# A sort's pieces placed anew, Exp for both router functions, and ScalarE multiplying more rows of a slot table

## The chip, the cores and the metric

The kernel runs on one core of a Trainium2 chip. The metric is the device time of one execution in microseconds (us); the median of several executions is given. A core has five engines that run side by side, each with a queue of its own that is worked off strictly in order: TensorE (PE: matmuls and transposes, results into PSUM), VectorE (DVE), ScalarE (ACT: functions and scaled copies), GpSimd (POOL) and SyncE (SP, which here issues DMAs). An engine waits on semaphores for what others produce. PSUM has eight banks of 128 x 512 float32; which matmul may start is often a matter of which bank has been read out.

## The reference, cut to what matters

One block: a layer norm of x (8 sequences of 512 tokens, 512 wide), then two branches on the normed tokens, whose results are multiplied and added to x.

```python
xn = _layernorm(x)
s = attention(xn)          # 16 heads of 32, chunks of 128, gated group norm, output matmul
g = silu(mixture(xn))      # 16 experts, 4 per token, and one shared expert
return x + s * g

# attention: q, k = rotate(silu(xn @ Wq)), rotate(silu(xn @ Wk)); v = xn @ Wv
#   per chunk: scores = (q @ k.T) * decay; o = scores @ v + (q * decay_q) @ state
#   o = o * sigmoid(xn @ Wg1 @ Wg2); o = o * rsqrt(mean(o*o per head) + eps) * weight; o @ Wo
# mixture:
probs = softmax(xn @ gate_w.T)
routing_weights, selected = top_k(probs, 4)
routing_weights /= routing_weights.sum(-1, keepdims=True)
for e in range(16):
    mixed += comb[:, e:e+1] * (silu(xn @ Wg[e]) * (xn @ Wu[e])) @ Wd[e]
mixed + swiglu_shared(xn) * sigmoid(xn @ shared_gate_w)
```

## The kernel before, in words

All is float32. The program is one long trace that is laid out in stages; a scheduler places each engine's instructions by its own estimate of when they become ready, except where the code ties an instruction behind an earlier one (`on_pe()` ties every matmul group of the first stages behind the one before, so PE's order is the order of the code; `behind(engine)` ties an instruction behind the engine's latest).

- **First pass** (`first`, sequences b = 0 to 7): norm, transposes (`turn`, psT L289), router logits (`route_1` to `route_3`: plT, pl, lg, the four largest, wt and the one-hot masks `mask`), and the shared expert (`share_1`: pg in bank m and pu in bank d, L355; `share_2`: pys L371, copied by ACT at L374 and stored). It is a generator. `along()` draws nine fifths of a piece each time it is called, so that the first pass runs between the steps of the attention of sequence 0. When its pieces end, the first piece of `sort` runs.
- **PSUM banks** are named by tags: a has four, d two, m one, k one. A tile of a tag takes the bank of that tag that was taken longest ago and waits until it has been read. Keys (`key`: pk L659, Silu at L669, rotation on DVE at L671 to L675) take m, queries take d, `value(b, t)` takes m for even t and d for odd t (pv L615, copied at L619), scores take the four a banks.
- **sequence(b)** is the attention of one sequence: for each of four groups of heads `scores` (pk of the states L714, ps L725, masked on DVE into sc at L750), `step()`, key of group g + 2 (or two value tiles of the next sequence), `by_token` (transposes of kT, L691, scaled by ACT into kd, L696), `step()`, query, `output` (po L766 and L772, multiplied on DVE at L776). After the groups: the last value tile, `squares` (ACT, PE's pr, square root rs), `inverse` (reciprocal on DVE, L794), keys and queries of the next sequence, `normed` (pb, on at L810), and for sequence 0 the output matmul `project` (pw L817, in bank d, copied by ACT into so at L1029). `also()` draws a piece of `sort` in sequence 0.
- **sort**: where each token's four rows go among the blocks of the experts. Piece 1: two matmuls (total, before) that sum the masks, L387. Piece 2: a scan and some thirteen small DVE instructions (L393 to L428). Piece 3: nine more (L432 to L450), which give `at`. Then four pieces, each a POOL product (oa, L456) and a DVE sum (pos, L458). The last piece makes posi and sp, the softmax weights wt (Exp on ACT, L470; product with the mask on POOL, L471; den and its reciprocal on DVE, L473 and L474; product on POOL, L475), and the Sigmoid of the shared gate sgs (L477), and stores them.
- **table**: turns positions into slots, in 8 groups of 16 lists. `make(i)` compares on DVE, in two halves of 8 lists: places (L526, 128 x 512 float16) and blocks (L529). The places must be multiplied by a token number: the first half on DVE in one instruction (L533), the second half by ACT, one instruction of 128 x 64 for each list (`number`, L542). Two homes hold two groups, so that a group is made while the one before it is used. PE multiplies 16 pairs per group into pn (L565, bank a), DVE adds pn to acc (L576, L574). `between[0]` draws a piece of the table after each matmul of sequence 1's keys, queries and values. The last part sums up pslot (L581), and DVE writes the slots (L586), by which POOL gathers rows for the expert blocks (L1153).
- **gate_2** makes the gate of the next `on` (p L645, four tiles in four banks; Sigmoid on ACT, L649). In sequence 1 it runs in group 0.
- Then come the expert blocks (304 to 692 us) and the attention of sequences 2 to 7 with the mixture.

Of the kernel before, what the change touches and what calls it, by code (L numbers as in the profile page):

```python
# [10 lines left out]
F32 = mybir.dt.float32  # L11
# [4 lines left out]
AF = mybir.ActivationFunctionType  # L16
ALU = mybir.AluOpType
AX = mybir.AxisListType
# [79 lines left out]
def tile_block(ctx: ExitStack, tc: tile.TileContext, a: dict, out: bass.AP):  # L98
# [8 lines left out]
    def bank(tag, name):  # L107
        return pp.tile([P, 512], F32, tag=tag, name=name, bufs={"a": 4, "k": 1, "m": 1, "d": 2}[tag])
# [110 lines left out]
    def behind(engine):  # L219

        last = next(
            (i for i in reversed(nc.cur_bb.bb.instructions) if i.engine == engine), None)
        return tc.issue_after(last) if last else nullcontext()
# [140 lines left out]
    def share_2(b):  # L364
        h = h1_of.pop(b)
        xT1_of.pop(b)
        for t in range(NC):
            sh = p1.tile([P, D], F32, tag="sh1", name=f"sh1_{b}_{t}", bufs=6)
            py = bank("dama"[t], f"pys_{b}_{t}")
            with on_pe():  # L370
                nc.tensor.matmul(  # L371
                    py, lhsT=h[:, t * P : (t + 1) * P], rhs=sw[:, KC * 2 * F :],
                    start=True, stop=True)
            nc.scalar.copy(sh, py)  # L374
            nc.sync.dma_start(sh_d[b][t * P : (t + 1) * P, :], sh)


    def sort():
# [5 lines left out]
        for to, by, name in ((total, ones, "total"), (af, tri, "before")):  # L384
            ps = bank("a", f"p{name}")
            with on_pe():
                nc.tensor.matmul(ps, lhsT=by, rhs=mf, start=True, stop=True)  # L387
            nc.scalar.copy(to, ps)
        yield
        incl = p1.tile([P, E, NT], F32, tag="incl", name="incl")  # L390
        fl = incl.rearrange("p e t -> p (e t)")
# [34 lines left out]
            nc.vector.tensor_scalar(end[:, 1], end[:, 1], float(2 * PAIRS), None, ALU.add)  # L426
        with behind(DVE):
            nc.vector.tensor_copy(filled, end[:, 1, E - 1 : E])  # L428
        yield

        with behind(DVE):
# [35 lines left out]
        with behind(DVE):  # L467
            nc.vector.tensor_copy(sp, bl.rearrange("p w r t -> p w (r t)"))

        nc.scalar.activation(wt, wt, AF.Exp)  # L470
        nc.gpsimd.tensor_tensor(wt, wt, mask.rearrange("p e t -> p t e"), ALU.mult)  # L471
        den = p1.tile([P, NT], F32, tag="den", name="den")
        nc.vector.tensor_reduce(den, wt, axis=AX.X, op=ALU.add)  # L473
        nc.vector.reciprocal(den, den)  # L474
        nc.gpsimd.tensor_tensor(  # L475
            wt, wt, den.unsqueeze(2).to_broadcast([P, NT, E]), ALU.mult)
        nc.scalar.activation(sgs, sgs, AF.Sigmoid)  # L477
        nc.sync.dma_start(sg_d, sgs)
        nc.sync.dma_start(
            xn_d[:, 2 * D :].rearrange("(t p) e -> p t e", p=P),  # L480
# [5 lines left out]
    def table(room):  # L486

        half = room.bitcast(F16)  # L490
        free = [0]
        quads = GROUP // QUAD


        def part(*shape):
            n = int(np.prod(shape))
            free[0] += n
            flat = half[:, free[0] - n : free[0]]
            return flat.rearrange("p (q j) -> p q j", j=QUAD) if len(shape) == 2 else (
                flat.rearrange("p (u q j) -> p u q j", u=quads, j=QUAD))  # L500

        homes = [(part(quads, HALF, QUAD), part(quads, 2 * NB, QUAD))]
        free[0] = 2 * WE * (LATE - LATE // 2)
        homes.append((part(quads, HALF, QUAD), part(quads, 2 * NB, QUAD)))

        def flat(n):
            free[0] += n
            return half[:, free[0] - n : free[0]]

        acc = flat(2 * NB)  # L510

        def rows(of, n):
            return of.rearrange("p (u j) -> p u j", j=QUAD).unsqueeze(2).to_broadcast(
                [P, of.shape[-1] // QUAD, n, QUAD])

        def make(i):
            place, block = homes[i // GROUP % 2]
            for u in range(0, quads, quads // 2):
                us = slice(u, u + quads // 2)
                lists = slice(i + u * QUAD, i + (u + quads // 2) * QUAD)  # L520

                def counts(n):
                    return count[:, :n].unsqueeze(1).to_broadcast([P, quads // 2, n, QUAD])

                with tc.issue_after(masked[0]) if i == GROUP and u == 0 else nullcontext():
                    nc.vector.tensor_tensor(  # L526
                        place[:, us], counts(HALF), rows(sp[:, 0, lists], HALF), ALU.is_equal)
                with tc.issue_after(masked[0]) if i == GROUP and u == 0 else nullcontext():
                    nc.vector.tensor_tensor(  # L529
                        block[:, us], counts(2 * NB), rows(sp[:, 1, lists], 2 * NB),  # L530
                        ALU.is_equal)
                if u == 0:
                    nc.vector.tensor_tensor(  # L533
                        place[:, us], place[:, us], rows(half_token[:, lists.start % NT :][
                            :, : GROUP // 2], HALF), ALU.mult)

        def number(i, some):
            place = homes[i // GROUP % 2][0]
            for j in range(max(some[0], GROUP // 2), some[1]):
                row = place[:, j // QUAD, :, j % QUAD]  # L540
                t = (i + j) % NT
                nc.scalar.activation(row, row, AF.Copy, scale=token[:, t : t + 1])  # L542

        yield
        make(0)
        for j in range(0, GROUP, 4):
            number(0, (j, j + 4))
            yield
        for i in range(0, TOPK * NT, GROUP):
            more = i + GROUP < TOPK * NT  # L550
            if more:
                make(i + GROUP)
            else:
                for e in range(E - LATE, E - LATE // 2):
                    nc.sync.dma_start(wexp[:, e, :], a["experts"][:, e, :])
            if i < TOPK * NT // 2:
                yield
            place, block = homes[i // GROUP % 2]
            pn = bank("a", f"pn_{i}")
            for some in ((0, 5), (5, 10), (10, GROUP)):  # L560
                if some[0] == 5:
                    with on_pe():
                        for j in range(GROUP):
                            h = j % 2 * HALF
                            nc.tensor.matmul(  # L565
                                pn[h : h + HALF, : 2 * NB],
                                lhsT=place[:, j // QUAD, :, j % QUAD],
                                rhs=block[:, j // QUAD, :, j % QUAD], start=(j < 2),
                                stop=(j >= GROUP - 2))
                if more:  # L570
                    number(i + GROUP, some)
                if some[1] == GROUP:
                    if i:
                        nc.vector.tensor_tensor(acc, acc, pn[:, : 2 * NB], ALU.add)  # L574
                    else:
                        nc.vector.tensor_copy(acc, pn[:, : 2 * NB])  # L576
                yield
        pt = bank("a", "pslot")
        with on_pe():
            for h in range(2):  # L580
                nc.tensor.matmul(  # L581
                    pt[h * HALF : (h + 1) * HALF, :NB], lhsT=fold,
                    rhs=acc.rearrange("p (b h) -> p b h", h=2)[:, :, h], start=True, stop=True)
        t = const.tile([P, NB], I32, tag="slot", name="slot")
        with behind(DVE):
            nc.vector.tensor_scalar(t, pt[:, :NB], float(B * N // 2), None, ALU.add)  # L586
        slots.append(t)
# [90 lines left out]
    def key(b, g, ps=None):  # L678
        kT_of[g] = rotated(b, g, "k", wk, ps)
# [113 lines left out]
    def inverse(b):  # L793
        nc.vector.reciprocal(rs_of[b], rs_of[b])  # L794
# [62 lines left out]
    def sequence(b, step, projected, before=None, defer=False, also=lambda: None):  # L857
# [10 lines left out]
        fill = ([0], [1], [2], [3], [], [], [], [])  # L868
        for g in range(G):
            scores(b, g)  # L870
            step()
            if g + 2 < G:
                key(b, g + 2)
            else:
                value(n, 2 * (g - 2))
            if g + 1 < G:
                by_token(b, g + 1)
            project_tiles(before, fill[2 * g])
            step()
            if g + 2 < G:  # L880
                query(b, g + 2)
                if g + 3 == G and n not in xT_of:
                    load_xT(n)
            if g + 2 == G:
                value(n, 1)
            if g == 0 and b not in on_of:
                gate_2(b)
            project_tiles(before, fill[2 * g + 1])
            if fill[2 * g + 1] == [NC - 1]:
                on_of.pop(before, None)  # L890
            output(b, g)
            if defer and g + 2 == G:
                gate_1(n)
            step()
# [18 lines left out]
        squares(b)  # L913
        step()
        inverse(b)
        key(n, 0)
        also()
        query(n, 0)
# [574 lines left out]
```

## Time and profile before

| what | us |
|---|---|
| timed runs, median of 3 (lowest, highest) | 1140.58 (1140.27, 1141.29) |
| the profiled execution's own time | 1134.81 |
| its span, first to last instruction | 1133.0 |
| PE busy in the span | 1106.5 |
| DVE busy | 737.3 |
| ACT busy | 428.6 |
| POOL busy | 447.2 |

TensorE's granted clock was 1.000 over the whole span. In the profile a line such as `L542 ACT ACTIVATE wexp<-wexp,token` names the line of the code, the engine, the operation and out<-in by tile names (buffer numbers are left out; the table lies in the memory of later expert weights and so is called wexp). In a timeline the first two columns are the start and the duration of a run of like instructions, the end tells their number, and brackets give the engine's idle time before them and what ended it. In a list of waits the three numbers are the total in us, how often, and the longest.

### The profile page before, as it was taken

The numbers are of one execution on the slowest core, as the hardware profiler recorded it, in microseconds if no ns is written. First come the engines' busy times: TensorE is split into PE (matmuls) and PEld (weight loads), VectorE is DVE, ScalarE is ACT, GpSimd is POOL, SyncE is SP. The second block draws the span as 40 slices with busy tenths as digits, with TensorE's granted clock in tenths as the row PEclk, the third lists the DMA queues.
The fourth block names the chain that finished last, engine by engine and source line by source line (L and its number), as shares of the span: only waits on it lengthen the run. The fifth ranks groups of instructions, "written<-read, shape, count | busy, mean of one in ns | idle before, by whom it ended". The sixth has DMA issues, their size and how long they took to land. (4 is left out here: it accounts for less than half of the span.)

```text
span 1133.0 us, 21299 instructions
## 1 busy us (share of the span) xinstructions
PE 1106.5 (98%) x7670; PEld 675.5 (60%) x7670; DVE 737.3 (65%) x1584; ACT 428.6 (38%) x924; POOL 447.2 (39%) x430
## 2 busy tenths in 40 slices
PE   7999999998999999999999999999999999999998
PEld 4445554455577777777777775655645555546453
DVE  6357744899344455444445446968889597797774
ACT  3223424264443333333333442353442522523541
POOL 4212100200333333333333323855877858858211
PEclk9999999999999999999999999999999999999999
DMA  9995342092789999989999975824647537444012
GB/s 341 326 319 191 143 151 48 22 383 70 239 201 234 244 236 241 240 237 239 237 240 249 256 204 216 292 81 142 232 121 236 177 113 258 143 136 142 19 38 75
DMA packets 163930, 218.48 MB, mean 193 GB/s; under 512 B 89840, under 2 KB 99184, under 8 KB 161776
## 3 DMA queue, kind: packets, MB, share of 16 engines
q1 hardware_dynamic: 142704, 146.76, 41.6%
q0 software_dynamic: 21120, 70.34, 23.4%
q8 instruction: 63, 1.03, 0.4%
q14 instruction: 43, 0.35, 0.1%
HBM read 126.78 MB, written 72.43 MB: 176 GB/s over the span
## 5 line engine op out<-in xcount | busy, mean ns | idle before, releaser
L1224 PE MATMUL pgu<-xts,wst 128*128 128x256 f32 x896 | 202.6, 379 | 0.0
L1224 PEld LDWEIGHTS pgu<-xts,wst 128*128 128x128 f32 x896 | 170.1, 190 | 46.2 <-issue 13.2
L1343 POOL DMA_INDIRECT yg<-y_d,place x128 | 142.8, 1115 | 30.3 <-issue 18.3
L1153 POOL DMA_INDIRECT more<-xn_d,slot x69 | 65.6, 951 | 216.6 <-DVE w L1207 113.8
L1255 PE MATMUL py<-wexp,slb 128*128 x272 | 129.9, 593 | 0.0
L1259 DVE TENSOR_SCALAR y<-py,w 128x512 f32<-128x512 f32 x136 | 102.0, 750 | 41.5 <-PE py L1255 34.8
L615 PE MATMUL pv<-wv,xT 128*128 128x512 f32 x256 | 118.2, 602 | 1.0 <-ACT sh L374 1.0
L659 PE MATMUL pk<-xT,wk 128*128 128x512 f32 x256 | 118.2, 603 | 0.0
L659 PE MATMUL pq<-xT,wq 128*128 128x512 f32 x256 | 115.7, 593 | 0.3 <-PEq L1307 0.3
L1236 ACT ACTIVATE slb<-pgu 128x256 f32<-128x256 f32 (+1 forms) x80 | 28.2, 352 | 222.7 <-PE pgu L1224 180.6
L1237 DVE TENSOR_TENSOR slb<-slb,pgu 128x256 f32<-128x256 f32 (+1 forms) x80 | 30.5, 381 | 121.1 <-ACT slb L1236 121.1
L817 PE MATMUL pw<-wo,on 128*128 128x512 f32 x224 | 100.6, 596 | 5.2 <-DVE m L1381 4.4
L1153 POOL DMA_INDIRECT xg<-xn_d,slot x67 | 63.7, 950 | 101.4 <-DVE w L1207 48.2
L1385 POOL TENSOR_TENSOR xo<-xo,m 128x512 f32<-128x512 f32 x31 | 45.3, 1462 | 128.1 <-DVE m L1381 120.9
L1186 ACT COPY xts<-pl 128x512 uint16<-128x512 uint16 x110 | 84.3, 769 | 2.4 <-DMA pl<-more 1.3
L750 DVE TENSOR_TENSOR sc<-ps,dmask 128x512 f32<-128x512 f32 x128 | 79.0, 676 | 1.0 <-PE ps L725 1.0
L659 PEld LDWEIGHTS pq<-xT,wq 128*128 128x128 f32 x256 | 47.2, 190 | 54.2 <-issue 52.7
L615 PEld LDWEIGHTS pv<-wv,xT 128*128 128x128 f32 x256 | 46.0, 190 | 51.3 <-issue 46.8
L659 PEld LDWEIGHTS pk<-xT,wk 128*128 128x128 f32 x256 | 46.2, 189 | 50.7 <-issue 48.3
L817 PEld LDWEIGHTS pw<-wo,on 128*128 128x128 f32 x224 | 41.2, 190 | 54.5 <-issue 45.2
L1205 DVE COPY wst<-wexp 128x512 f32 x112 | 43.2, 426 | 37.0 <-DVE y L1259 15.7
L1255 PEld LDWEIGHTS py<-wexp,slb 128*128 128x128 f32 x272 | 45.5, 191 | 27.4 <-issue 26.8
(196 smaller groups left out, 1713.1 us busy)
## 6 DMA issues: line engine op xcount, KB each, us to landing
y_d<-y SPq DMA_DIRECT2D x136, 256.0 KB, 4.1
wexp<-in_experts SPq DMA_DIRECT2D x16, 768.0 KB, 5.0
sh_d<-sh SPq DMA_DIRECT2D x32, 256.0 KB, 3.5
xT<-xT_d SPq DMA_DIRECT2D x8, 1024.0 KB, 6.7
m<-sh_d SPq DMA_DIRECT2D x32, 256.0 KB, 4.6
xo<-in_x SPq DMA_DIRECT2D x32, 256.0 KB, 2.8
out<-xo SPq DMA_DIRECT2D x31, 256.0 KB, 2.0
x<-in_x SPq DMA_DIRECT2D x7, 1024.0 KB, 8.8
```

The lines of the kernel that those rows point to most:

```text
L615: nc.tensor.matmul(pv, lhsT=xT_of[b][:, k, t * P : (t + 1) * P], rhs=wv[:, k, :], start=(k == 0), stop=(k == KC - 1))
L659: nc.tensor.matmul(ps, lhsT=w[:, k, g * P : (g + 1) * P], rhs=xT_of[b][:, k, :], start=(k == 0), stop=(k == KC - 1))
L750: masked[:] = [nc.vector.tensor_tensor(s, pss[j].rearrange("p (c t) -> p c t", t=C), dmask[:, g * HG + j].unsqueeze(1).to_broadcast([P, NC ...
L817: nc.tensor.matmul(pw, lhsT=on_of[b][:, g, t * P : (t + 1) * P], rhs=wo[:, g, :], start=(g == 0), stop=(g == G - 1))
L1153: nc.gpsimd.indirect_dma_start(out=row(i), out_offset=None, in_=xn_d, in_offset=bass.IndirectOffsetOnAxis(ap=slot[:, i : i + 1], axis=0))
L1186: (nc.vector.tensor_copy if j in by_dve else nc.scalar.copy)(xt[:, u, KP:, :].bitcast(U16).rearrange("p k (t h) -> p h k t", h=2), pls[j % ...
L1205: nc.vector.tensor_copy(to, wflat[:, bass.ds(off + u * KC * F, KC * F)])
L1224: nc.tensor.matmul(pg[:, o * 2 * P : (o + 1) * 2 * P], lhsT=wst[j % 2][k // KP][:, (k % KP * 2 + o) * F :][:, :F], rhs=xt[:, :, k, :], sta ...
L1255: nc.tensor.matmul(py, lhsT=hT[:, u * P : (u + 1) * P], rhs=wflat[:, bass.ds(off + KC * 2 * F, D)], start=True, stop=True)
L1259: gone.append(nc.vector.tensor_scalar(y, py, w[:, u : u + 1], None, ALU.mult).ins)
L1343: nc.gpsimd.indirect_dma_start(out=yg, out_offset=None, in_=y_d, in_offset=bass.IndirectOffsetOnAxis(ap=place[:, r, g : g + 1], axis=0))
L1385: nc.gpsimd.tensor_tensor(xo, xo, m, ALU.add)
```

## The change

- `share_2` takes its banks in the order m, d, a, a instead of d, a, m, a.
- In `sequence`, `step()` after `scores` stays where it is for b > 0; for b = 0 it moves behind the key or value. For b = 1 the step does nothing. `gate_2` of sequence 1 puts its fourth tile in bank m instead of a.
- One more `also()` in front of the next sequence's key, behind `inverse`; it does something in sequence 0 alone, where it draws the sort's piece behind the scan.
- In `sort`, the two copies of piece 1 are tied to ACT's order, and the Exp of wt moves there, with an Exp of -sgs in place of the Sigmoid. Mask product, den, reciprocal, sgs + 1, its reciprocal and the product with 1/den move to the end of piece 2.
- In `table`, DVE multiplies the first half of the places in group 0 alone; for the other seven groups ACT multiplies all 16 lists (120 instructions instead of 64).

```diff
@@ share_2
-            py = bank("dama"[t], f"pys_{b}_{t}")
+            py = bank("mdaa"[t], f"pys_{b}_{t}")
@@ sort
-            nc.scalar.copy(to, ps)
+            with behind(ACT):
+                nc.scalar.copy(to, ps)
+        with behind(ACT):
+            nc.scalar.activation(wt, wt, AF.Exp)
+        with behind(ACT):
+            nc.scalar.activation(sgs, sgs, AF.Exp, scale=-1.0)
         yield
...
             nc.vector.tensor_copy(filled, end[:, 1, E - 1 : E])
+        nc.gpsimd.tensor_tensor(wt, wt, mask.rearrange("p e t -> p t e"), ALU.mult)
+        den = p1.tile([P, NT], F32, tag="den", name="den")
+        with behind(DVE):
+            nc.vector.tensor_reduce(den, wt, axis=AX.X, op=ALU.add)
+        with behind(DVE):
+            nc.vector.reciprocal(den, den)
+        with behind(DVE):
+            nc.vector.tensor_scalar(sgs, sgs, 1.0, None, ALU.add)
+        with behind(DVE):
+            nc.vector.reciprocal(sgs, sgs)
+        nc.gpsimd.tensor_tensor(
+            wt, wt, den.unsqueeze(2).to_broadcast([P, NT, E]), ALU.mult)
         yield
...
-        nc.scalar.activation(wt, wt, AF.Exp)
-        nc.gpsimd.tensor_tensor(wt, wt, mask.rearrange("p e t -> p t e"), ALU.mult)
-        den = p1.tile([P, NT], F32, tag="den", name="den")
-        nc.vector.tensor_reduce(den, wt, axis=AX.X, op=ALU.add)
-        nc.vector.reciprocal(den, den)
-        nc.gpsimd.tensor_tensor(
-            wt, wt, den.unsqueeze(2).to_broadcast([P, NT, E]), ALU.mult)
-        nc.scalar.activation(sgs, sgs, AF.Sigmoid)
         nc.sync.dma_start(sg_d, sgs)
@@ table, make and number
-                if u == 0:
+                if i == u == 0:
                     nc.vector.tensor_tensor(
                         place[:, us], place[:, us], rows(half_token[:, lists.start % NT :][
                             :, : GROUP // 2], HALF), ALU.mult)
...
-            for j in range(max(some[0], GROUP // 2), some[1]):
+            for j in range(max(some[0], 0 if i else GROUP // 2), some[1]):
@@ sequence
             scores(b, g)
-            step()
+            if b:
+                step()
             if g + 2 < G:
                 key(b, g + 2)
             else:
                 value(n, 2 * (g - 2))
+            if not b:
+                step()
...
-                gate_2(b)
+                gate_2(b, banks="aaam" if b else "aaaa")
...
         inverse(b)
+        also()
         key(n, 0)
```

## The prediction

> **What bounds the kernel now.** I read the windows first, then TensorE's (PE's) waits, then the timelines of the places that the diff touches. All times are us of the profile of before, counted from the span's start. The windows (columns: busy time and instructions of each engine, then clock, DMA share, GB/s):
>
> ```profile
> core 0: us, PE busy (x) PEld busy (x) DVE busy (x) ACT busy (x) POOL busy (x), PEclk, DMA share, GB/s
> ...
> 89.00:187.00 98.00, 95.08 (x777) 50.93 (x776) 60.89 (x210) 36.90 (x78) 13.02 (x18) 1.00 0.42 151
> 187.00:227.00 40.00, 40.00 (x235) 18.78 (x233) 31.05 (x66) 12.47 (x23) 8.53 (x7) 1.00 0.13 25
> 227.00:283.50 56.50, 52.07 (x708) 30.91 (x707) 54.21 (x99) 30.33 (x95) 0.00 (x0) 1.00 0.60 228
> ```
>
> PE is busy nearly throughout, so only its idle time can be won. From 227 to 283.5 (sequence 1 with the slot table) DVE is as full as PE. ScalarE (ACT) has room, but its queue is in order. PE's waits up to 304 us, by what released them:
>
> ```profile
> PE pn L565 <- DVE sc L750: 3.1, 2, 2.3
> PE p L645 <- DVE wexp L576: 1.4, 1, 1.4
> PE psT L289 <- DVE sc L750: 1.0, 1, 1.0
> PE pv L615 <- ACT sh L374: 1.0, 1, 1.0
> PE pg L355 <- ACT sh L374: 0.9, 1, 0.9
> PE pl L318 <- DVE sc L750: 0.8, 1, 0.8
> ```
>
> Four small waits of sequence 0 and three of sequence 1: some 7 us in all. ACT and DVE where the table begins:
>
> ```profile
> 217.00 0.59 ACT L1029 COPY so<-pw 128x512 f32<-128x512 f32 x1 [3.38 <-PE pw L817]
> 220.39 0.59 ACT L1029 COPY so<-pw 128x512 f32<-128x512 f32 x1 [2.80 <-PE pw L817]
> 227.08 2.52 ACT L542 ACTIVATE wexp<-wexp,token 128x64 f16<-128x64 f16 x10 [6.10 <-DVE wexp L526]
> 229.48 0.56 ACT L1029 COPY so<-pw 128x512 f32<-128x512 f32 x1
> ```
>
> ```profile
> 214.08 1.10 DVE L673 TENSOR_TENSOR kT<-sk,cos 128x512 f32<-128x512 f32 x1
> 215.11 1.75 DVE L674 TENSOR_TENSOR swk<-swk,sin 128x512 f32<-128x512 f32 x1
> ...
> 226.58 0.42 DVE L526 TENSOR_TENSOR wexp<-count,sp 128x512 f16<-128x512 f16 x1
> ```
>
> The first two copies of the projection leave their banks at once; ACT's rows of the table wait until DVE has compared the second half of group 0 (end 227.0). A row costs 2.52/10 = 0.25 us. Two DVE multiplies that usually last 0.68 last 1.10 and 1.75 while POOL multiplies (210.88 to 216.31).
>
> **The change, part by part.** Orders and waits are read off the changed program's queues, durations off the rows.
>
> *Bank m first in share_2, sequence 0.* pys_0 now takes bank m. For x_1 it follows pv_2, also in m: pv starts at 42.98, its copy ends at 46.62 + 0.59 = 47.21, so pys starts at 47.25 instead of 46.52 (+0.73). The wait of pg at 54.6 goes: from pys to pg are 7.97 us of work, so pg starts at 55.22 instead of 55.49: net -0.27. For x_2 pys_0 follows pk (64.32, also m); its Silu ends at 67.96 + 0.60 = 68.56, pys starts at 68.60 instead of 67.76: +0.84. The other six passes have other work between two users of m.
>
> *step() behind key or value.* In groups 0 and 1 pk now stands directly before pg, both in m: pk's 3.60, 0.10 to ACT, 0.60 of Silu, 0.03 back is 4.33, against 3.50 from start to next start: +0.83, twice. In group 2 pv_0 stands before the transposes, which wait for sc: from ps (152.75) to the transpose of kT (160.66) were 7.91, now 1.15 + 3.50 + 1.75 = 6.40: -1.5. In group 3 from ps (178.12) to ptotal (188.40) were 10.28, now 1.1 + 3.5 (pv_2) + 0.83 (pys_0 waits for v's copy) + 3.47 = 8.9: -1.35. Its cover is the mask: 2.9 us from lg to mask (181.72 to 184.62), ready 1.1 before ptotal. Without that cover the gain shrinks by what is missing. DVE's and SP's queues are reordered as well (kT before h, xT's load before the halves): nothing behind them is due sooner than before, apart from xT of b=1, which landed 6 us early and keeps about 3. Sum: -0.27 + 0.84 + 1.66 - 1.5 - 1.35 = **-0.6**.
>
> *Sort.* Exp for the gate saves one table load (1.28) in ACT time that waits for PE anyway: nothing. The softmax moves behind pbefore; squares start some 1.0 us later against PE and are read 0.3 later still: nothing, up to +0.5 if that cover fails. DVE gets den (0.69 + 0.35, which before lay in idle time) and sgs + 1 with its reciprocal (nearest rows: small DVE instructions of 0.17, reciprocal 0.35; 0.4 to 0.7, I take 0.6) ahead of rs. Nine instructions of the third piece now use DVE's idle time behind the reciprocal. From on's last product (192.22) to the end of the second comparison (227.0) before: 34.8, of which 1.02 + 2.03 + 0.64 idle and 1.6 stretched by POOL: 29.5 of work. Now 31.2, no idle time (all feeders come sooner), plus POOL: its four products fall on kT, swk and kT's sum, 0.4 to 1.1 extra each by the two rows above, so 1.5 to 3.2, I take 2.3; wt's product under the scan 0 to 0.8, I take 0.4. So 33.9 from 191.60: the comparison ends at **225.5** (224.3 to 226.8), 1.5 sooner than before. SP's store of posi now stands ahead of so's: PE waits for neither.
>
> [...]
>
> *ScalarE's rows.* DVE loses seven multiplies of 0.42 (0.34 from start to start): 2.4 us. ACT gains 56 rows of 0.25: 14 us, put among its other work. Two places decide:
>
> 1. The copy of pw's second tile now stands behind three rows of group 0, which wait for the comparison: 225.5 + 0.1 + 3 x 0.25 + 0.59 = 226.95. The fourth tile needs that bank (d). It started at 213.22 + 3 x 3.48 = 223.66; now 226.95: PE is **3.3 late** (2.1 to 4.6). Behind it in PE's queue stands all of sequence 1.
> 2. gate_2's fourth tile in bank m ends the wait of 1.36 (it stretched p2 from 1.10 to 3.16: -2.06). But ACT now reaches the Sigmoids late. ps_0 230.76; four sc from 232.1 to 234.5; comparison 234.9; ACT: five rows 236.2, Silu of k 236.8, four kd 237.75, three rows; DVE: kT's four instructions and the next comparison 239.8; ACT: five rows 241.1, Silu of q 241.7, ten rows 244.2, table load 1.28, 245.45. The first Sigmoid ends at 246.0, the third at 247.05. PE wants these banks for ps_1 at 243.7; ps_1 ends at 247.9 instead of 244.8: +3.1. Net +1.0: **4.3 late** at pk_3 (247.9, was 243.59).
>
> *To the slots.* DVE's product with po_0 needs all Sigmoids (247.6). From there to sc_3 were 29.04 (244.47 to 273.51); less 4 x 0.34 of removed multiplies, plus 0.75 of waits for pn_16 and kT_3: sc_3 at 276.05, pn_80 at 276.7 (was 274.25). The table's wait of 2.31 is thus partly won back. 9.1 later come the slots, 285.8 against 283.3: **+2.5**. ACT's last sixteen rows end at 283.5, pn_112 wants them at 283.65: just covered.
>
> Behind the slots all five queues are unchanged, PE is filled, and the delay reaches the end: span 1133.0 + 2.5 = 1135.5. The profiled run took 1134.81 and the timed runs 1140.58 in the median; carrying that difference: **1143.1**.
>
> **The rivals.**
>
> - *Rows ready before the copies (faster).* ACT's queue was laid out as if the comparison ended before pw's second copy (about 220). If it does, both places of ACT lose their price: no 3.3, no 3.1, and DVE's saving counts. PE then loses only its bank waits: -0.6 - 5.4 (what the three waits of sequence 1 cost with their stretches) + 1 = -5: 1135.6. It decides if the comparison ends 5 us sooner than I work out. For: the windows leave ACT 26 us. Against: DVE's sum of 31.2 without any POOL stretch still ends at 222.8. Chance 0.13.
> - *One place only (no change).* If POOL stretches little (ends 223.3), the fourth tile waits 2 less: +0.5, 1141.0; likewise if rows run under the copies. Chance 0.35.
> - *ACT bounds the table's end.* Its cover of 0.15 at pn_112 is thin; 1.5 us more in its queue goes straight to the slots: 1144.6. For: 120 rows of 0.25 in 57 us beside 14 us of other work, each gated by DVE. Against: sixteen rows are 4.1 us, a group has 7. Chance 0.18.
> - *It doesn't do what it says*: the old DVE multiply is guarded by i, ACT's rows by the same i; the queues show 120 rows against 64. No chance kept.
>
> **How the numbers follow.** Forecast (1142 to 1144) 0.34 with ACT's case 0.18 gives slower 0.52; no change 0.35; faster 0.13. 0.2% (2.3 us) is about what a measurement of this kernel tells from no change, and the forecast lies just beyond it. The range reaches from inside the fast case to the upper bound of the comparison (+4.6): 1138.7 to 1145.2.
>
> **What would show it.** In the new profile: PE waits at pw (L817's tile 4) for ACT's so by 3 to 4 us; at ps for the Sigmoids by 2 to 3 us; at pg twice and at pys three times by 0.7 each; none at psT, pl; p2 without a wait. The second comparison of group 0 ends at 224.3 to 226.8. Slots at 285 to 286.5. Wrong if the so copy isn't late, or if PE's order behind the slots runs shorter.

## The result and the profile after

| | us |
|---|---|
| timed runs after, median of 20 (lowest, highest) | 1149.11 (1141.98, 1154.12) |
| timed runs before, median of 20 on the same chips | 1138.14 (1135.89, 1144.14) |
| ratio, 95% interval | 1.0099, 1.0087 to 1.0111 |
| profiled run after, its span | 1147.96, 1146.1 |
| profiled run before, its span | 1134.81, 1133.0 |

The change makes the kernel about 11 us slower; forecast were 2.5, with a range that ended at 1145.2. Lines of after are 9 higher in the table and the attention than those of before (L817 is now L826) and 13 higher in the block part (L1029 is now L1042); in the kernels of the experiments they shift by a few again.

TensorE's waits between 10 and 306 us, the four largest (columns as before: total, how often, longest):

```profile
PE pw L826 <- ACT so L1042: 4.3, 1, 4.3
PE pg L355 <- ACT sk L678: 2.8, 2, 2.0
PE ps L734 <- ACT on L658: 1.6, 1, 1.6
PE pn L574 <- DVE sc L759: 1.4, 1, 1.4
```

Of the six waits of before that the prediction lists, one for sc is left, and new ones for ScalarE stand in their place: the projection's second copy, the Sigmoids, and a Silu (twice); three at pys of 0.6 to 0.7 each are smaller. They are waits that the prediction named. ScalarE's queue shows the first: three rows of the table, which waited for VectorE, stand ahead of the copy.

```profile
228.41 0.84 ACT L551 ACTIVATE wexp<-wexp,token 128x64 f16<-128x64 f16 x3 [9.13 <-DVE wexp L535]
229.14 0.56 ACT L1042 COPY so<-pw 128x512 f32<-128x512 f32 x1
```

All waits of this stretch add up to 13.6 us, those of before to 9.5. That is 4 us more, so the waits can't make 13 us by themselves. TensorE's timeline shows the rest, first after, then the same places before:

```profile
214.92 10.57 PE L826 MATMUL pw<-wo,on 128*128 128x512 f32 x24
229.76 6.67 PE L826 MATMUL pw<-wo,on 128*128 128x512 f32 x8 [4.27 <-ACT so L1042]
236.36 0.40 PE L723 MATMUL pk<-v,kd 128*32 128x32 f32 x24
...
251.70 2.94 PE L734 MATMUL ps<-qT,kT 32*128 32x128 f32 x30 [1.57 <-ACT on L658]
254.57 3.66 PE L668 MATMUL pk<-xT,wk 128*128 128x512 f32 x6
```

```profile
213.22 14.00 PE L817 MATMUL pw<-wo,on 128*128 128x512 f32 x32
...
242.47 1.19 PE L725 MATMUL ps<-qT,kT 32*128 32x128 f32 x32
243.59 2.84 PE L659 MATMUL pk<-xT,wk 128*128 128x512 f32 x6
```

Three tiles of the projection take 10.57, that is 3.5 each; the fourth, behind the wait, takes 6.67 for the same eight passes. Behind the second wait 30 small passes take 2.94 (32 took 1.19 before) and six passes of pk 3.66 (2.84 before). The windows show why. I laid windows 3.41 us wide, on the places where the clock changes (start:end, length, PE busy, the other engines, then clock, DMA share, GB/s):

```profile
225.53:228.94 3.41, 0.00 (x0) 0.00 (x0) 2.97 (x5) 0.53 (x3) 0.12 (x1) 1.00 0.73 229
228.94:232.36 3.42, 2.60 (x3) 1.18 (x4) 2.24 (x3) 3.42 (x15) 0.41 (x1) 0.50 0.99 392
232.36:235.77 3.41, 3.41 (x5) 1.35 (x4) 0.00 (x0) 0.96 (x3) 0.00 (x0) 0.50 0.79 266
249.42:252.83 3.41, 1.83 (x38) 1.22 (x34) 2.56 (x5) 3.38 (x7) 0.00 (x0) 1.00 1.00 355
252.83:256.25 3.42, 3.42 (x28) 2.35 (x29) 2.83 (x6) 0.53 (x2) 0.00 (x0) 0.50 0.99 376
```

Behind 225.53 to 228.94, where TensorE was idle throughout, its granted clock is 0.50 from 228.94 to 235.77, two windows, with 0.82 of idle time in the first of them. Behind 249.42 to 252.83, where it was idle for 1.58, the clock is 0.50 from 252.83 to 256.25. A third stretch at 0.50, from 1017.42 to 1020.83, follows a wait of 1.91 for the mixture's m that before has as well, at full clock behind it; first after, then before:

```profile
1016.09 5.40 PE L826 MATMUL pw<-wo,on 128*128 128x512 f32 x8 [1.91 <-DVE m L1394]
```

```profile
1005.66 3.70 PE L817 MATMUL pw<-wo,on 128*128 128x512 f32 x8 [1.91 <-DVE m L1381]
```

The sum of the profiled run, against before: 1.1 up to ptotal (189.53 against 188.40), 0.7 more up to the fourth tile, 4.27 of wait and 3.07 of slow tile: ps_0 is 9.2 late (236.68, was 227.48). From there to the slots (pslot at 293.61, was 283.32; forecast 285.8) it takes 1.1 more, in which 2.6 of half clock outweigh what the other waits save. Behind the slots come 0.1, the third stretch with 1.7 (5.40 against 3.70), and 0.9 at 1064 us, where a square root's matmul waits for Sigmoids that POOL's chain held up; 13.1 in all. About 7.4 of this is half clock (3.07, 2.6 and 1.7).

The granted clock of each timed run fits this: 0.992 to 0.996 in 19 of 20, and 0.999 in the one run that took 1141.98, only 3.8 over the median of before.

### The profile page after: what moved, and what is told of

The parts are those of the page before. It is cut to its first block, busy times and chain, and to the rows that moved or that the text cites. A ratio compares the mean times of both kernels' runs of the same rounds, so it can differ in the third digit from the quotient of the medians.

```text
span 1146.1 us, 21376 instructions
## 1 busy us (share of the span) xinstructions
PE 1114.7 (97%) x7670; PEld 679.3 (59%) x7670; DVE 742.4 (65%) x1579; ACT 439.2 (38%) x979; POOL 448.0 (39%) x430
## 5 line engine op out<-in xcount | busy, mean ns | idle before, releaser
L826 PE MATMUL pw<-wo,on 128*128 128x512 f32 x224 | 105.5, 620 | 9.4 <-DVE m L1394 4.4
L1166 POOL DMA_INDIRECT xg<-xn_d,slot x67 | 63.6, 949 | 99.7 <-DVE w L1220 55.6
L826 PEld LDWEIGHTS pw<-wo,on 128*128 128x128 f32 x224 | 42.9, 198 | 61.6 <-issue 47.4
L743 ACT COPY blocked<-state 32x96 f32<-32x96 f32 x96 | 30.7, 320 | 84.4 <-DVE state L738 83.5
```

Source lines behind the costliest of these rows:

```text
L826: nc.tensor.matmul(pw, lhsT=on_of[b][:, g, t * P : (t + 1) * P], rhs=wo[:, g, :], start=(g == 0), stop=(g == G - 1))
L1166: nc.gpsimd.indirect_dma_start(out=row(i), out_offset=None, in_=xn_d, in_offset=bass.IndirectOffsetOnAxis(ap=slot[:, i : i + 1], axis=0))
```

## The experiments

All ratios are to the kernel before, timed on the same chip in the same set. "The two ties" are orders on ScalarE's queue, nothing else: the first puts the table's rows of group 0 behind the projection's second copy, the second puts the rows of groups 2 to 7 behind the Sigmoids of sequence 1. The table leaves out the ladder, which is told below:

| run | what it is | us | before | ratio (95%) |
|---|---|---|---|---|
| so_first | changed, first tie | 1145.75 | 1137.82 | 1.0068 (1.0047 to 1.0090) |
| no_table | changed, table part undone | 1148.95 | 1137.82 | 1.0097 (1.0080 to 1.0114) |
| no_seq0 | changed, sequence 0 undone | 1143.96 | 1137.82 | 1.0049 (1.0032 to 1.0065) |
| late_copy | before, one late copy | 1140.88 | 1138.57 | 1.0016 (1.0000 to 1.0031) |
| sig_first | changed, two ties | 1140.85 | 1138.57 | 1.0015 (0.9997 to 1.0033) |
| split_only | before, step moved in two groups | 1135.60 | 1138.57 | 0.9970 (0.9953 to 0.9987) |
| best1 | two ties, step in two groups, old banks | 1134.00 | 1138.57 | 0.9964 (0.9944 to 0.9984) |
| best_aaaa | best1, gate without bank m | 1148.40 | 1150.96 | 0.9986 (0.9963 to 1.0009) |
| best_dve | best1, VectorE's multiplies | 1149.22 | 1150.96 | 0.9984 (0.9959 to 1.0009) |
| split_rows | split_only, rows behind Sigmoids | 1146.24 | 1150.96 | 0.9955 (0.9931 to 0.9979) |
| g1_back | changed, group 1's step undone | 1160.12 | 1151.17 | 1.0080 (1.0053 to 1.0108) |

The last four ran on chips where the kernel before takes some 12 us more; only their ratios and their traces can be set beside the others.

**so_first.**

```diff
@@ number
+                with tc.issue_after(copies[1]) if i == 0 else nullcontext():
                     nc.scalar.activation(row, row, AF.Copy, ...)
```

> The changed kernel, with ScalarE's rows of group 0 tied behind the copy of the projection's second tile; nothing else. Theory (the order of ScalarE's queue, and the slow clock behind the wait that it makes): the fourth tile of the projection starts at once and takes 3.6 us instead of 4.27 of wait and 6.67; ps_0 near 229.4 instead of 236.7; the Sigmoids may come 1.5 to 3 us late as before or a little later. Time 1139.5 to 1143.5. Rival A (56 more rows on ScalarE are the price, wherever they stand): over 1147. Rival B (the moves in sequence 0 are the price): over 1147.

The wait is gone, four tiles take 14.00, ps_0 comes at 230.49 (the first pass started 1.3 later than in the changed kernel's run). But the time, 1145.75, fits neither side: it lies above the theory's range and below the rivals'. The trace shows why:

```profile
216.24 14.00 PE L829 MATMUL pw<-wo,on 128*128 128x512 f32 x32
...
248.36 3.05 PE L737 MATMUL ps<-qT,kT 32*128 32x128 f32 x30 [4.02 <-ACT on L661]
```

The same loss stands one place later: since TensorE is no longer held up, it meets the Sigmoids 4.02 early instead of 1.57, and the clock is 0.50 from 246.60, within this wait, to 253.43. One tie alone moves the wait.

**no_table.** `if u == 0` and `GROUP // 2` are put back.

> The changed kernel with the table part undone: VectorE multiplies the first half of all groups again, ScalarE 64 rows. The three rows of group 0 still stand ahead of the projection's second copy. Theory: the wait at the fourth tile stays at 3.5 to 4.5 us with a slow tile behind it, the wait for the Sigmoids is gone, VectorE's seven multiplies are back: 1144 to 1149. Rival A (the rows themselves): the whole loss is gone, 1137 to 1140.

As the theory said. The wait at the fourth tile is 4.26, that for the Sigmoids is gone, and VectorE's waits return (2.31 and 0.82), the first with a half-clock stretch behind it (283.34 to 286.75). So the table part is not what puts rows ahead of the projection's copy. They are group 0's rows, whose number the diff leaves as it was, and no_seq0 has them there too: of the change's parts the sort's is left, which the scheduler takes to be done sooner. That last step is by elimination; the sort was not undone alone, so it is not shown.

**no_seq0.** `"dama"`, and `step()` in front of the key or value.

> The changed kernel with its parts in sequence 0 undone (banks d, a, m, a in share_2; the step in front of the key or value again). Theory: ptotal near 188.4 instead of 189.5, the wait at the projection's fourth tile stays at 3.5 to 5 us with a slow tile behind it: 1146.5 to 1150. Rival B (sequence 0 is the price): 1138 to 1142.

The wait is there (4.27), but the time, 1143.96, fell below the theory's range, though not to rival B's. Sequence 0 is a price of its own. Counted from the same start (the second pg, at 34.80 here, 34.09 in the changed kernel, 34.26 before), ptotal is 2.5 earlier than with the moves and 1.2 earlier than before. The last number is a gain of the sort's part alone that the prediction had at nothing: before, a table load and the Sigmoid of sgs stood between two copies of pys and made pv wait 1.04; that wait is not in this run. The rest of the difference to the changed kernel is a half-clock stretch of 3.41 behind the wait (227.95 to 231.36, the tile took 5.38) in place of one of 6.83. Why all four runs came out near 1144 stays open: their clocks are 0.997 three times and 0.993 once, at one and the same time.

**ladder.** Idle copies in front of the join of twelve pairs of expert blocks.

```diff
@@ join
+        for _ in range({6: 10, 10: 11, ... 50: 21}.get(j, 0)):
+            with behind(ACT):
+                nc.scalar.copy(xt[:, 0], sin...)
         nc.scalar.copy(xt[:, :, :KP, :]..., pt_of.pop(j)...)
```

> The kernel before, with idle copies on ScalarE (10, 11, ... 21 of 128x512, 0.54 us from start to start) put in front of the join of every fourth pair of expert blocks, so that TensorE waits there by about 0.54 N - 5.4 us: 0 to 6 us, 36 us in all; the copies write what the join overwrites. Theory (a wait above some 1.5 us halves TensorE's clock for 3.4 us or more): 7 to 9 of the twelve waits are followed by 16 passes that take 4.5 us or more instead of 3.62, time 1188 to 1198. Rival (the slow tile came from the expert loads that run beside it): all passes behind the waits at 3.62, clock 1.00, time 1172 to 1176.

The ladder was badly built: the copies also held up the neighbouring blocks' Silu, so no wait grew beyond 2.19. The time, 1175.67, lies in the rival's range, but its two runs (1171.90 and 1179.44) are 7.5 apart and so few waits were long enough that it decides nothing. Its windows do. Three of the twelve places are followed by half clock; here is the highest idle time at these places that was followed by full clock, and one that was not:

```profile
537.60:541.01 3.41, 1.51 (x8) 0.98 (x6) 0.28 (x2) 3.25 (x7) 1.03 (x2) 1.00 0.90 291
541.01:544.43 3.42, 3.34 (x16) 2.96 (x16) 0.43 (x1) 1.08 (x3) 0.00 (x0) 1.00 0.45 130
...
564.91:568.32 3.41, 1.33 (x6) 1.20 (x7) 0.00 (x0) 2.60 (x5) 0.00 (x0) 1.00 0.53 195
568.32:571.73 3.41, 3.41 (x10) 2.67 (x9) 0.43 (x1) 0.42 (x1) 0.91 (x1) 0.50 0.47 93
```

1.90 us idle in the first of these windows was followed by full clock, 2.08 in the other by 0.50, and 1.83 at the third place (619.52 to 622.94) by 0.50 too, so this idle time alone does not tell which comes. The theory's 1.5 was an estimate, from the wait of 1.57 in the changed kernel; no run shows such a limit. The rival, that the expert loads slow TensorE, falls: in the stretch at half clock the DMA share is 0.47, in one of full clock 0.90.

**late_copy.** The kernel before, with one copy made late.

```diff
@@ spill
+        if (b, t) == (0, 1):
+            for _ in range(14):
+                with behind(ACT):
+                    nc.scalar.copy(s, sin)
-        nc.scalar.copy(s, pw)
+        with behind(ACT) if (b, t) == (0, 1) else nullcontext():
+            copies.append(nc.scalar.copy(s, pw).ins)
@@ number
+                with tc.issue_after(copies[1]) if i < 2 * GROUP else nullcontext():
```

> The kernel before, with 14 idle copies on ScalarE in front of the copy of the projection's second tile (into the tile that this copy then overwrites), and the rows of groups 0 and 1 tied behind it, so that TensorE waits for that copy as in the changed kernel: 3.8 to 4.8 us at the fourth tile, and nothing else of the change. Theory (the wait costs itself and then halves the clock for one or two stretches of 3.41 us): the tile takes 5.3 to 6.7 instead of 3.6, the clock is 0.50 behind the wait, ps_0 comes 5.5 to 8 late; VectorE may work ahead meanwhile and win back up to 2 us of its own waits: 1142 to 1146. Rival (a wait costs itself alone): tile at 3.6, 1139.5 to 1142.5.

The wait came out at 1.99, half of what I meant: in this program the fourth tile takes the bank of the third, and the third's copy stands behind eleven of the idle copies (218.13 to 225.16 on ScalarE), not behind all fourteen. It still tells the theories apart:

```profile
225.79 5.40 PE L820 MATMUL pw<-wo,on 128*128 128x512 f32 x8 [1.99 <-ACT so L1037]
```

The tile takes 5.40 behind a wait of 1.99, and the clock is 0.50 from 226.11 to 229.52. ps_0 is 3.96 late (231.44, was 227.48): nothing of the change is in this kernel, and in this execution a wait of 2 us costs 4. The timed runs cost less than that: their median is 2.3 over before, below the theory's range and inside the rival's, and the profiled run is the slowest of the ten. So it is the trace, and not the time, that speaks for the theory here. The trace also has a second half-clock stretch, from 277.31 to 280.72, behind a wait of 2.30 at pn; the same wait is 2.31 in before, at full clock behind it.

**sig_first.** The first tie, and rows of groups 2 to 7 behind the last Sigmoid of sequence 1.

```diff
@@ number
+                at = copies[1] if i == 0 else gates[-1] if i >= 2 * GROUP else None
+                with tc.issue_after(at) if at else nullcontext():
```

> The changed kernel with two ties on ScalarE: group 0's rows behind the projection's second copy, and the rows of groups 2 to 7 behind the four Sigmoids of sequence 1. Theory (order of ScalarE's queue, not its load): neither the wait at the projection nor the one for the Sigmoids, clock 1.00 from 190 to 300 us, slots near 285; 1138.5 to 1141.5, that is 4 to 7 less than with the first tie alone. Rival A (the 56 rows themselves): another wait of 2 us or more for rows in front of a pn, over 1143.

As the theory said, and rival A falls: ScalarE works off the same 120 rows, and the loss shrinks from 11 us to 2.3 with an interval that reaches below 1. No wait for ScalarE is left between 190 and 306 us, and the clock is 1.00 in both windows:

```profile
190.00:230.00 40.00, 39.71 (x247) 18.45 (x248) 34.33 (x68) 15.27 (x29) 10.32 (x7) 1.00 0.19 49
230.00:286.00 56.00, 52.28 (x705) 31.23 (x702) 51.46 (x92) 42.61 (x150) 0.35 (x1) 1.00 0.58 225
```

The slots come at 286.20, a little behind the 285 expected. Counted from the second pg they are 2.0 behind before's, and 1.3 of that is there at ptotal already: it is sequence 0's.

**split_only.** `step()` behind the value in groups 2 and 3 of sequence 0 only.

> The kernel before with one edit: in sequence 0 the step stands behind the value tile in groups 2 and 3 only (groups 0 and 1 keep it behind the scores). The two terms of the prediction, 1.5 and 1.35 us, by themselves: ptotal at 185.5 instead of 188.4, time 1134.5 to 1136.5. Rival (the waits only move to the mask or to another bank): ptotal at 187.5 or later, no change.

The gain that the prediction saw there is real and larger: ptotal at 186.30, with a first pass that starts 1.5 later than in before (second pg at 35.77 against 34.26), so 3.6 from the same start. From ps to ptotal group 3 now takes 8.19 (before 10.28).

**g1_back.** `if b or g == 1: step()` in front of the key.

> The changed kernel with the step of group 1 of sequence 0 in front of the key again; groups 0, 2 and 3 as changed. In the changed kernel's trace group 1's pg waits 2.02 instead of the 0.83 of the prediction, because the load of Silu's table (1.28) stands directly before the key's Silu and starts only when pk has ended; before, the load came at once behind lT's copy. Theory: pg of group 1 starts without a wait and Silu's load comes early again; ptotal 1.8 to 2.1 earlier than the changed kernel's 189.5, counted from the same start; the wait at the projection's fourth tile stays at 4.2 to 4.3 with a slow tile behind it, so the time falls by about 2 to 3 us at most, to 1145 to 1148 where before takes 1138. Rival (the wait moves to the transposes that now follow pu): ptotal at 189 or later.

Group 1's pg no longer waits, and from the same start ptotal comes 1.7 earlier than in the changed kernel (188.24 - 0.42). By its ratio it can't be told from the changed kernel (1.0080 against 1.0099, with intervals that overlap). ScalarE's timelines show what doubled that wait; first the changed kernel, then the kernel before:

```profile
128.55 1.28 ACT L678 ACT_TABLE_LOAD   x1 [4.92 <-PE pk L668]
129.84 0.60 ACT L678 ACTIVATE sk<-pk 128x512 f32<-128x512 f32 x1
```

```profile
122.02 1.28 ACT L359 ACT_TABLE_LOAD   x1
126.88 0.60 ACT L359 ACTIVATE sl<-pg 128x512 f32<-128x512 f32 x1 [3.57 <-PE pg L355]
```

Before, the load of Silu's table ran in idle time, 4.9 ahead of its Silu. In the changed kernel the first Silu behind the Sigmoids is the key's, and its load waits for pk with it: 1.28 more on the path.

**best1 and three variants.** best1 has the two ties, `"dama"` and the step of split_only.

> All that the runs so far speak for: the changed kernel with both ties on ScalarE, share_2's banks in the old order, and the step behind the value only in groups 2 and 3. Theory: ptotal 185 to 186, slots at 278 to 280 instead of 283.3, no half clock before 300 us: 1132 to 1135. Rival A (rows): 1138 or more.

It beats the kernel before by its interval. ptotal is at 184.76, slots at 280.73 (forecast 185 to 186 and 278 to 280). But it does not beat split_only, which has one edit of it: the ratios are 0.9964 and 0.9970 in the same set, and counted from the second pg the slots come at 246.5 in best1, 245.4 in split_only and 249.1 in before. So the step alone accounts for the gain, and nothing here shows that the change's other parts add to it:

> The best kernel so far (best1) with one part of the change undone: gate_2 of sequence 1 takes four banks a again instead of a, a, a, m. If bank m only moved the wait (in best1 ps_1 waits 0.75 for pn_0's bank and takes 2.65 instead of 1.17; before, p waited 1.36 and took 1.1 + 0.7): slots within 0.5 us of best1's 280.7, time 1133 to 1135. If bank m is a gain as predicted (2.06): slots 1.5 to 2 later, 1135.5 to 1137.

> The best kernel so far (best1) with the table part undone: VectorE multiplies the first half of all groups, ScalarE 64 rows. If the rows on ScalarE are worth what VectorE loses (7 x 0.34 = 2.4 us): slots 1.5 to 2.5 later than best1's 280.7, time 1135.5 to 1137. If they are worth nothing because VectorE's free time appears as another wait: slots within 0.7, 1133 to 1135.

> split_only (the kernel before with the step behind the value in groups 2 and 3) with ScalarE's rows for all lists of groups 2 to 7 only, tied behind the Sigmoids of sequence 1 and group 0's behind the projection's second copy; sort, bank and gate as before the change. Theory (rows are free where they follow the Sigmoids; VectorE loses 6 x 0.34 = 2.0): slots 1 to 2 earlier than split_only's 281.2 from the same start, 1133 to 1135. Rival (VectorE's place is taken by another wait): as split_only, 1135 to 1137.

On that chip the expected times can't hold, and the three ratios can't be told from best1's by their intervals; I compare from ps_0 to the slots: before 55.84, best1 56.34, best_aaaa 57.30, best_dve 58.95, split_only 55.82, split_rows 54.45. best_aaaa and best_dve each have one half-clock stretch in there (1.7, half of its 3.41), so without it 55.6 and 57.2. The first of these stretches (240.21 to 243.63) follows a wait of 2.78 at p, the second (273.09 to 276.50) one of 2.32 at pn. So bank m is worth 1.0 as measured, less than nothing without the stretch, and in neither case the forecast 2.06: in best1 part of the wait that p had now stands at ps_1.

```profile
238.16 2.65 PE L738 MATMUL ps<-qT,kT 32*128 32x128 f32 x32 [0.75 <-DVE wexp L588]
```

ScalarE's rows are worth some 0.9 there (57.2 against 56.34; 2.6 with the stretch), and 1.4 in split_rows (54.45 against 55.82, neither with a stretch), of the 2.4 and 2.0 that VectorE is spared; the rest probably comes back as its other waits. split_rows has the shortest way from ps_0 to the slots and needs neither the sort's part nor the gate's. Whether it or best1 is faster isn't settled, since they never ran on one chip.

## Why the prediction was wrong

**The mechanism was right, the price of a wait was not.** The prediction held that ScalarE's in-order queue would be late at two places, and it was. It priced each wait as idle time only. "PE is 3.3 late" should have read: 4.27 late, and then 3.07 more for a tile at half clock. This step, a wait taken at its own length, is the one that failed. Over the profiled run it left out 7.4 of 13.1; late_copy's trace shows it with nothing else changed, and sig_first that with the two waits gone most of the loss goes (1.0015 instead of 1.0099). The second miss is sequence 0, 1.9 from the forecast by the same start.

Point by point:

- *Second comparison and the fourth tile.* Forecast 225.5 from on's product at 191.60; measured 228.33 from 193.35. The sum between, 33.9, measured 35.0. Of the difference, 0.4 is the stretch of the multiplies by POOL's four products, 2.7 (1.07, 0.45, 0.11 and 1.07 over the usual 0.68) where I took 2.3. The larger part, 0.75, is wt's product, where I took 0.4: while POOL makes it (194.05 to 196.50), the small instruction behind the scan takes 1.32 (195.21 to 196.53; 0.17 before). The start was 1.75 later, which is all sequence 0.
- *Sequence 0.* Forecast -0.6, measured +1.1, or +1.3 from the same start. Bank waits at pys (0.57 and 0.69) and group 0's pg (0.75) were as forecast (0.73, 0.84, 0.83); group 2 took 6.39 of 6.40, group 3 9.02 of 8.9. Group 1's pg waited 2.02 instead of 0.83, which is the table load; that group's loss alone is 1.45 more than forecast. "Exp ... nothing" was wrong in a place that I didn't look at: the old Sigmoid's load made pv wait 1.04 in group 3, so that part of group 3's gain belonged to the sort, which removes this wait by itself (no_seq0). In split_only the two groups gave 3.6, not 2.85, since pys_0 in its old bank doesn't wait for v.
- *Sigmoids.* Forecast 3.1 late; measured 1.57, where TensorE itself was 9.2 late by then. so_first shows 4.02 when it isn't. The wait was cheaper than said, the clock behind it dearer.
- *"ACT bounds the table's end"*: no. pn_112 came without a wait; the last wait is pn_80's for sc, 1.44, as before but shorter.
- *Rows ready before the copies*: no, the comparison ended at 228.33.
- *A sum that was off.* The six listed waits of before add up to 8.2, not some 7. No term of the forecast uses this sum.
- *Behind the slots all is unchanged*: true of the queues, false of the time. A stretch at half clock (1.7) and a wait of 0.9 were added there. Why the wait of 1.91 is followed by half clock here and by full clock in before is not shown.
- *The range.* It took in the bounds of each cost that I saw as unknown. The speed behind a wait was not among them, though before has a wait of 2.31 at full clock that I could have asked about.

## What to carry to other kernels

Price a wait of TensorE as its length plus what the clock may do behind it: here 1.7 us for 3.41 us at half clock (5.40 against 3.70 for the same eight passes). In these traces each of the five waits of 4 us (4.27 in the changed kernel and in no_seq0, 4.26 in no_table, 4.02 in so_first, 4.3 in g1_back) had 3.41 or 6.83 at half clock behind it. Waits of about 1.6 to 2.8 us went either way: 1.57 in the changed kernel, 1.99 in late_copy and 2.78 in best_aaaa had half clock behind them, 2.02 at pg in the changed kernel and 2.31 at pn in before did not. The changed kernel's shorter ones, 1.4 at pn and less, cost themselves. When an engine's queue is put in order by a scheduler, look for instructions that wait for something late and stand ahead of a copy that frees a bank: the fix is an order, not less work. Removing one such wait exposes the next, so tie both before judging.

## What the runs showed of the hardware

- The stretches at 0.50 named here lasted 3.41 us or 6.83: in the changed kernel 228.94 to 235.77, 252.83 to 256.25 and 1017.42 to 1020.83, in so_first 246.60 to 253.43, in no_table 228.73 to 235.56 and 283.34 to 286.75, in no_seq0 227.95 to 231.36, in late_copy 226.11 to 229.52 and 277.31 to 280.72, in best_aaaa 240.21 to 243.63, in best_dve 273.09 to 276.50, in g1_back 227.81 to 234.63, 251.70 to 255.11 and 729.56 to 736.39, in the ladder 568.32 to 571.73, 595.63 to 599.04 and 622.94 to 629.76.
- The same wait had full clock behind it in one run and half clock in another: at pn 2.31 in before, 2.30 in late_copy and 2.32 in best_dve, full clock behind the first alone; for the mixture's m 1.91 in before (full) and in the changed kernel (half). What makes the difference is not shown.
- The wait of 4.27 had 6.83 at half clock behind it in the changed kernel, where 0.82 of the first 3.41 were idle, and 3.41 in no_seq0, where none of it was.
- Among small passes (32 x 128 and the like) half clock followed 3.41 us with 1.58 idle in the changed kernel (249.42 to 252.83), 1.62 in g1_back (248.28 to 251.70) and 1.42 in g1_back (726.15 to 729.56, most of it in gaps of 0.46 to 0.48); full clock followed 3.41 us with 1.43 in no_seq0 (245.02 to 248.43). Whether small passes matter for it was not tried by itself.
- On the chips where before takes 1151 us, short passes of the mixture's stage come in bursts with gaps that the profile puts down to issue (in split_rows 4.3 us in pk, 9 gaps, and 1.9 in ps, 8 gaps; in best_dve 3.3 and 1.6). The profiles of before, the changed kernel, late_copy, sig_first, split_only and best1, on other chips, have no wait of TensorE that is put down to issue. Where the gaps come from was not looked into.
